# Folding softmax sums over partition quarters: a small product on TensorE, or two copies through DRAM

## The chip, the core and the metric

The kernel runs on one NeuronCore of a Trainium2 chip. The metric is the device time of one execution in microseconds (us); lower is better. PE is TensorE (matrix products), DVE VectorE, ACT ScalarE, POOL GpSimd, and SP is SyncE, which here issues nearly all of the copies between DRAM and on-chip memory.

## What is computed

Two layers over 16 batches of 1024 nodes with 256 channels, all in float32. Layer 0 is graph-weighted attention, layer 1 a two-step graph convolution; each ends in a residual sum and a layernorm. Cut to the first layer, for one batch:

```
c_adj = mean(x, channels)                          # one number for each node
A     = abs(abs(sigmoid(c_adj[m] - c_adj[n]) - 0.5) - 0.5) * 2
g     = relu((x.T @ (adj * A)) * para)             # 256 x 1024: the queries
k, v  = split(x @ kv_w)                            # 4 heads of 64 channels
attn  = softmax(q @ k.T * scale, axis=keys)
x     = layernorm(x + attn @ v)
```

and of the second layer

```
h = relu(x @ w1_loop + adj @ (x @ w1_neigh) + b1)
h = relu(h @ w2_loop + adj @ (h @ w2_neigh) + b2)
x = layernorm(x + (x + h) * 0.5)
```

The change is in the softmax's denominators, that is in the sums of exponentials over the keys.

## The kernel before, in words

A loop over the batches b = 0 to 15 (line 990) works on several batches at once: while batch b is in attention, the queries, keys and values of batch b + 1 are prepared, the first graph step of batch b - 1 and the second of batch b - 2 are done together (class Joined, lines 860 to 931), and batch b - 3 is normalized and stored. Batches 3 to 14 are all alike. Batch 0 and 1 lack the earlier batches, batch 2 lacks b - 3, and batch 15 has no next one. The order on every engine is the order of the calls (`tc.manual_schedule`, line 1159); no scheduler moves anything.

Attention goes in four units for each batch: a pair of heads and a half of the 1024 query nodes each. For a unit u:

- `scores(u)` (lines 586 to 607): eight times PE makes a tile of 128 keys by 2 x 512 scores (line 594), ACT takes the exponentials (597), and DVE adds the tile to `acc` (601, 603). DVE then transposes `acc` in blocks of 32 x 32 (605) and sums over 32 columns (607). This leaves `den_part`, 128 x 32: each denominator is still spread over four groups of 32 partitions, the quarters.
- `outputs(u)` (609 to 618): PE multiplies the exponentials with the values (614); DVE transposes the result to `o` (618).
- `add(u)` (620 to 639): PE multiplies `den_part` with the constant `fold`, which adds the four quarters and copies the sum to all of them (626); DVE takes two reciprocals from PSUM (630), multiplies `o` by them (632), adds the result to the residual `xB` (634) and sums it for the layernorm (635).

What lies between the units is written out by hand in `gap0`, `gap1`, `gap2` (lines 1005 to 1044). In the alike batches it is this, in the order of the calls:

- after unit 0, gap0: `means` (line 256) has ACT sum the next batch's nodes; the 1024 means go to DRAM as one line of 4-byte elements (263). `c1.inner` is a product (712). Then `add(0)`. SP loads the node form of batch b - 2 (`x<-x1d`, 705) and four blocks of a far adjacency form (`both.fetch(2, 3)`, line 181), POOL forms the operands R (882 to 885), and `row()` (268) reads the line of means back, broadcast to all partitions. DVE transposes the next batch's `xB` to `xT` (219).
- after unit 1's scores, DVE forms the key sums K (384 to 387).
- after unit 1, gap1: SP loads two row blocks of `adj` (443) and four more far blocks (`both.fetch(1, 4)`). `both.run` makes seven groups of products (892) in the order 1, 2, 6, 7, 5, 4, 3, with hooks between them: after group 2 DVE adds p1 (911) and does `add(1)`; after group 6 come a likeness on ACT (459, 460) and on DVE the moments of batch b - 3 (275, 276); after group 5 `weigh_first` on DVE (465, 518 to 521); after group 4's products DVE adds `uT` (925). The PSUM tile that line 925 reads is needed again by the second scores tile of unit 2.
- after unit 2, gap2: `c2.last` (780, 782 on PE; 787, 790 on DVE), then `add(2)`.
- after unit 3 the queries' products (546) with `add(3)` inside, then keys and values.

All of SP's copies of this part are on one queue. An instruction of SP that waits holds up all behind it. There are eight completion semaphores, used in turn: a copy is issued only once the copy eight places before it has landed.

Of the kernel before, what the change touches and what calls it, by code (L numbers as in the profile page):

```python
# [10 lines left out]
F32 = mybir.dt.float32  # L11
I32 = mybir.dt.int32
AF = mybir.ActivationFunctionType
ALU = mybir.AluOpType
AX = mybir.AxisListType
# [3 lines left out]
def kernel(  # L19
# [31 lines left out]
    nc = tc.nc  # L51

    B, N, C = x.shape
    P = 128
# [3 lines left out]
    HD = C // HEADS  # L58
    HID = w1_loop.shape[1]
    FB = 512  # L60
# [9 lines left out]
    S = 32  # L70
    NB = N // S
# [3 lines left out]
    Q = P // S  # L75
# [4 lines left out]
    small = ctx.enter_context(tc.tile_pool(name="small", bufs=4))  # L80
    psum = ctx.enter_context(tc.tile_pool(name="psum", bufs=2, space=bass.MemoryType.PSUM))

    dram = ctx.enter_context(tc.tile_pool(name="dram", bufs=2, space=bass.MemoryType.DRAM))
# [7 lines left out]
    def bank_psum(name):  # L91
        return psum.tile([P, FB], F32, tag="bank", name=name, bufs=2)
# [6 lines left out]
    def row_tile(name):  # L99
        return work.tile([P, N], F32, tag="row", name=name, bufs=ROWS)  # L100
# [15 lines left out]
    for t0 in range(0, NT, 2):  # L116
        nc.sync.dma_start(out=x_first[:, t0:t0 + 2, :],
                          in_=x[0, t0 * P:(t0 + 2) * P, :].rearrange("(t p) c -> p t c", p=P))
# [42 lines left out]
    fold = const.tile([P, Q, S], F32, name="fold")  # L161
# [14 lines left out]
    def fetch(n, name):  # L176

        rows = []
        for h in range(2):
            rows.append(row_tile(f"adj_{n}_{name}_{h}"))  # L180
            nc.sync.dma_start(out=rows[h], in_=far_adj[n][h])
        return rows

    def store(n, rows):
        for h in range(2):
            nc.sync.dma_start(out=far_adj[n][h], in_=rows[h])
# [28 lines left out]
    def channel_major(blocked, name):  # L215

        dst = work.tile([P, NC, N], F32, tag="xT", name=name, bufs=2)
        for cc in range(NC):
            nc.vector.transpose(dst[:, cc, :], blocked[cc])
        return dst  # L220
# [26 lines left out]
    def fold_sums(part, name):  # L247

        pm = bank_psum(f"{name}_ps")
        nc.tensor.matmul(pm[:, 0:NB], fold.rearrange("p a k -> p (a k)"), part[:, 0, :], start=True, stop=True)  # L250
        return pm[:, 0:NB]

    def join(part):
        nc.vector.tensor_add(part[:, 0, :], part[:, 0, :], part[:, 1, :])

    def means(q, xb, name):

        c_col = small.tile([P, NT], F32, tag="c_col", name=f"c_col_{name}", bufs=2)
        for t in range(NT):
            nc.scalar.activation(xb[:, t, :], xb[:, t, :], AF.Identity, accum_out=c_col[:, t:t + 1])  # L260
        nc.gpsimd.tensor_scalar_mul(c_col, c_col, 1.0 / C)
        line = dram.tile([1, N], F32, tag="line", name=f"line_{name}")
        nc.sync.dma_start(out=line.rearrange("o (t p) -> p (o t)", p=P), in_=c_col)
        q.c_col = c_col

        def row():
            q.c_row = work.tile([P, N], F32, tag="c_row", name=f"c_row_{name}")
            nc.sync.dma_start(out=q.c_row, in_=line.to_broadcast([P, N]))

        return row  # L270
# [24 lines left out]
    def by_node(t):  # L295
        return t.rearrange("p (bn r) -> p bn r", r=S)

    class BlockedNorm:


        def __init__(self, xB, sums, name):
            self.xB, self.sums, self.name = xB, sums, name

        def mean(self):
            mean = small.tile([P, NB], F32, tag="mean", name=f"mean1_{self.name}", bufs=2)
            nc.vector.tensor_scalar_mul(mean, fold_sums(self.sums, f"sum1_{self.name}"), 1.0 / C)
            for cc in range(NC):
                x_cc = by_node(self.xB[cc])
                nc.vector.tensor_sub(x_cc, x_cc, mean.unsqueeze(2).to_broadcast([P, NB, S]))  # L309
# [262 lines left out]
    class Attention:  # L572
# [5 lines left out]

        def __init__(self, b, xB, qT, kT, v):
            self.b, self.xB, self.qT, self.kT, self.v = b, xB, qT, kT, v  # L580
            self.part, self.o = {}, {}

            self.rden = small.tile([P, len(UNITS) * FB // S], F32, tag="rden", name=f"rden_{b}", bufs=2)
            self.sums = small.tile([P, NC, NB], F32, tag="sums", name=f"sums_{b}", bufs=2)
# [24 lines left out]
        def outputs(self, u):  # L609
# [7 lines left out]
            self.o[u] = work.tile([P, FB], F32, tag="o", name=f"o_{b}_{u}")  # L617
            nc.vector.transpose(self.o[u], pav)

        def add(self, u):  # L620

            b, (pair, j) = self.b, UNITS[u]
            half = FB // S
            pd = bank_psum(f"den_ps_{b}_{u}")
            den = pd[:, 0:2 * half]
            nc.tensor.matmul(den, fold.rearrange("p a k -> p (a k)"), self.part.pop(u), start=True, stop=True)
            rden = self.rden[:, ts(u, half)]
            for s in range(2):
                rows = slice(s * HD, (s + 1) * HD)
                nc.vector.reciprocal(rden[rows, :], den[rows, ts(s, half)])  # L630
            o = by_node(self.o.pop(u))
            nc.vector.tensor_mul(o, o, rden.unsqueeze(2).to_broadcast([P, half, S]))
            dst = by_node(self.xB[pair][:, ts(j, FB)])
            nc.vector.tensor_add(dst, dst, o)
            nc.vector.tensor_reduce(self.sums[:, pair, ts(j, half)], dst, AX.X, ALU.add)
            if u == len(UNITS) - 1:
                join(self.sums)
                nc.vector.tensor_reduce(rden_min[:, b:b + 1], self.rden, AX.X, ALU.min)
                nc.vector.tensor_reduce(rden_max[:, b:b + 1], self.rden, AX.X, ALU.max)
# [293 lines left out]
    def run():  # L933
# [56 lines left out]
        for b in range(B):  # L990
            more = b + 1 < B
            att = Attention(b, xB, qT, kT, v)
            c1, c2, c3 = (convs.get(b - k) for k in (1, 2, 3))
            both = Joined(c1, c2) if c2 else None
# [10 lines left out]
            def gap0():  # L1005
                row = means(q, xb, str(b + 1))
                c1.inner()
                att.add(0)
                if both:
                    c2.load_x()  # L1010
                    both.fetch(2, 3)
                    both.left(nc.gpsimd)
                row()
                ready["xT"] = channel_major(blocked, f"xT_{b + 1}")

# [5 lines left out]
            def gap1():  # L1021
                for t in (0, TJ):
                    q.load(t)
                if both:
                    both.fetch(1, 4)
                    both.run({1: (lambda: q.left(nc.gpsimd),),
                              2: (lambda: att.add(1),),
                              6: (lambda: q.likeness(0), lambda: c3 and c3.moments()),
                              7: (lambda: q.likeness(TJ),),
                              5: (weigh_first,),  # L1030
                              4: (lambda: c3 and c3.finish(out[b - 3]),),
                              3: (c1.turn_blocks,)})
                else:
                    q.left(nc.gpsimd)
                    for t in (0, TJ):
                        q.likeness(t)
                    store("01", rows01)
                    c1.first(rows01, lambda: (att.add(1), adj_sums(rows01, 1), adj_sums(rows01, 2), weigh_first()))
                    c1.turn_blocks()

            def gap2():
                if both:
                    c2.last()
                att.add(2)

            between = [gap0, gap1, gap2] if c1 and more else []
            if more:
                q = (FastQueries if c1 else Queries)(b + 1, xb)
            for u in range(len(UNITS)):
                att.scores(u)  # L1050
                if u == 1 and between:
                    kv = KeysValues(b + 1, ready["xT"])
                    kv.sums()
                if u == 3 and between:
                    for t in (2, TJ + 2, 3, TJ + 3):
                        q.load(t)
                    for t in (2, TJ + 2, 3, TJ + 3):
                        q.likeness(t)
                    q.right(1)
                if u and not between:  # L1060
                    att.add(u - 1)
                att.outputs(u)
                if u == 2 and more:
                    if c1:
                        for t in (1, TJ + 1):
                            q.load(t)
                            q.likeness(t)
                            q.times_adj(t)
                    else:
                        for t in range(3):  # L1070
                            q.load(t)
                            q.weigh(t)
                if u < 3 and between:
                    between[u]()
                if u == 0 and more and not between:
                    means(q, xb, str(b + 1))()
# [67 lines left out]
        both = Joined(c1, c2)  # L1144
# [83 lines left out]
```

## Time and profile before

| | us |
|---|---|
| median of 3 runs | 2168.85 (2168.66 to 2168.91) |
| the profiled execution's own time | 2169.0 |
| its span, from first to last instruction | 2167.2 |
| PE busy | 2153.0 (99%), in 8054 records |
| DVE busy | 1888.0 (87%) |
| ACT busy | 1033.0 (48%) |
| POOL busy | 367.3 (17%) |
| copies, mean | 132 GB/s, the queue of SP 54.9% of 16 engines' time |
| mean granted PE clock | 0.998 |

A float32 product is recorded as two instructions, so `x128` of line 626 are 64 calls. A row of the timeline gives the start, the time up to the end of the last merged instruction, the engine, the line and what is written from what; where an engine was idle before it, that and the releaser stand in brackets. A waiting SP is not idle in that sense: its waits are a view of their own. Matmul ends are modelled, so the time from one start to the next is the safer measure on PE. The time that a batch takes in the alike batches is 133.2 us, from the first scores at 801.32 to those at 934.52.

### The profile page before, as it was taken

How to read it: one execution, taken by the hardware profiler on the slowest of the kernel's cores; microseconds unless marked ns; L12 is line 12 of the kernel's file. 1: busy time of each engine (PE TensorE's matmuls, PEld its weight loads, DVE VectorE, ACT ScalarE, POOL GpSimd, SP SyncE). 2: the span in 40 equal slices, each digit the busy share in tenths (PEclk: the TensorE clock that was granted, in tenths of full speed). 3: DMA queues.
4: the chain of work that ended last, by engine and by line, in shares of the span. 5: the costliest groups of instructions: out<-in, count | busy, mean ns of one | idle time of the engine just before them, and what ended most of it. 6: DMA issues, size and time to landing. Idle time of an engine off the chain costs nothing.

```text
span 2167.2 us, 23089 instructions
## 1 busy us (share of the span) xinstructions
PE 2153.0 (99%) x8054; PEld 1024.8 (47%) x8054; DVE 1888.0 (87%) x2336; ACT 1033.0 (48%) x1356; POOL 367.3 (17%) x211
## 2 busy tenths in 40 slices
PE   9999999999999999999999999999999999999998
PEld 5344444544444444444444445454454444544354
DVE  5978998898998989989889888999989899898964
ACT  4744545545355453445444454445543445535412
POOL 1011130211303113030120301203022130221021
PEclk9999999999999999999999999999999999999999
DMA  9393663746556365473655536566374653743442
GB/s 240 107 136 117 135 161 99 132 140 118 146 128 152 112 125 156 125 170 95 115 163 124 163 88 115 172 122 155 98 114 163 122 156 109 121 152 82 120 136 99
DMA packets 611770, 286.21 MB, mean 132 GB/s; under 512 B 504768, under 2 KB 569152, under 8 KB 611648
## 3 DMA queue, kind: packets, MB, share of 16 engines
q1 hardware_dynamic: 611376, 284.15, 54.9%
q8 instruction: 65, 1.06, 0.2%
q14 instruction: 57, 0.47, 0.1%
q10 hardware_dynamic: 272, 0.52, 0.1%
HBM read 238.16 MB, written 46.46 MB: 131 GB/s over the span
## 4 chain that ended last, share of the span: by engine, by line


## 5 line engine op out<-in xcount | busy, mean ns | idle before, releaser
L597 ACT ACTIVATE pr<-s 128x1024 f32<-128x1024 f32 x512 | 476.1, 1051 | 176.6 <-PE s L594 176.6
L603 DVE TENSOR_TENSOR acc<-acc,pr 128x1024 f32<-128x1024 f32 x384 | 494.2, 1287 | 41.1 <-DVE acc L603 1.0
L594 PE MATMUL s<-qT,kT 64*128 64x512 f32 x2048 | 457.1, 596 | 0.7 <-ACT qT L480 0.7
L614 PE MATMUL av<-pr,v 128*64 128x512 f32 x2048 | 453.6, 595 | 0.0
L594 PEld LDWEIGHTS s<-qT,kT 64*128 64x128 f32 x2048 | 191.1, 186 | 236.1 <-ACT pr L597 111.5
L614 PEld LDWEIGHTS av<-pr,v 128*64 128x64 f32 x2048 | 141.2, 137 | 300.2 <-issue 285.8
L326 POOL TENSOR_TENSOR rstd<-rstd,neg_half 128x32 f32<-128x32 f32 x16 | 87.1, 5441 | 1111.5 <-DVE rstd L324 1111.5
L459 ACT ACTIVATE wg<-c_row,c_col 128x1024 f32<-128x1024 f32 x128 | 146.9, 1148 | 70.3 <-DVE accB L605 51.2
L465 DVE SCALAR_TENSOR_TENSOR wg<-wg,adj 128x1024 f32<-128x1024 f32 x128 | 149.8, 1209 | 11.3 <-ACT wg L460 10.4
L892 PE MATMUL hu_ps<-adj,R 128*128 128x512 f32 x360 | 158.3, 596 | 0.0
L460 ACT ACTIVATE wg<-wg 128x1024 f32<-128x1024 f32 x128 | 135.4, 1058 | 4.1
L314 ACT ACTIVATE sq<-xB_a 128x1024 f32<-128x1024 f32 x32 | 33.8, 1057 | 194.3 <-DVE xB_a L309 193.1
L360 PE MATMUL v_ps<-kvw_sb,xT 128*128 128x256 f32 x512 | 120.2, 379 | 0.1
L546 PE MATMUL g_ps<-wg,S 128*128 128x512 f32 x224 | 116.7, 603 | 0.0
L360 PEld LDWEIGHTS v_ps<-kvw_sb,xT 128*128 128x128 f32 x512 | 97.2, 190 | 38.4 <-issue 21.0
L546 PE MATMUL g_ps<-T,S 128*128 128x512 f32 x224 | 114.4, 592 | 0.0
L546 PE MATMUL g_ps<-wg,x 128*128 128x512 f32 x224 | 109.0, 599 | 0.0
L892 PE MATMUL hu_ps<-adjT,t 128*128 128x512 f32 x240 | 105.7, 592 | 0.0
L892 PEld LDWEIGHTS hu_ps<-adj,R 128*128 128x128 f32 x360 | 67.3, 190 | 78.9 <-issue 76.5
L601 DVE TENSOR_TENSOR acc<-pr,pr 128x1024 f32<-128x1024 f32 x64 | 76.9, 1201 | 23.7 <-ACT pr L597 23.7
L605 DVE STREAM_TRANSPOSE accB<-acc 128x1024 f32<-128x1024 f32 x64 | 79.7, 1246 | 3.2
L908 ACT COPY snap<-hu_ps 128x512 f32<-128x512 f32 x15 | 8.8, 586 | 150.3 <-PE hu_ps L892 150.3
(189 smaller groups left out, 2917.0 us busy)
## 6 DMA issues: line engine op xcount, KB each, us to landing
adj<-in_adj_dram SPq DMA_DIRECT2D x128, 512.0 KB, 3.9
adj<-adjT SPq DMA_DIRECT2D x120, 512.0 KB, 10.2
para<-in_L_gnn_para_dram SPq DMA_DIRECT2D x32, 512.0 KB, 3.4
xB_a<-in_x_dram SPq DMA_DIRECT2D x128, 128.0 KB, 4.2
x1d<-xB_a SPq DMA_DIRECT2D x128, 128.0 KB, 3.4
x<-x1d SPq DMA_DIRECT2D x16, 1024.0 KB, 16.6
xB<-in_x_dram SPq DMA_DIRECT2D x120, 128.0 KB, 4.3
x<-in_x_dram SPq DMA_DIRECT2D x15, 1024.0 KB, 6.9
```

What stands on the lines that cost most here:

```text
L326: nc.gpsimd.tensor_tensor(self.rstd, self.rstd, neg_half, ALU.pow)
L360: nc.tensor.matmul(pv[:, ts(i, C)], xT[:, cc, ts(g * per + i, P)], kvw_sb[:, cc, C:2 * C], start=(cc == 0), stop=(cc == NC - 1))
L459: nc.scalar.activation(wg, self.c_row, AF.Abs, bias=self.c_col[:, t:t + 1], scale=-1.0)
L460: nc.scalar.activation(wg, wg, AF.Tanh, scale=-0.5)
L465: nc.vector.scalar_tensor_tensor(wg, wg, 1.0, self.adj.pop(t), op0=ALU.add, op1=ALU.mult)
L546: nc.tensor.matmul(self.p[n], x_n[:, k, :], w_n, start=(k == 0), stop=(k == TJ - 1))
L594: nc.tensor.matmul(ps[:, ts(s, FB)], self.kT[rows, pair, ts(mt, P)], self.qT[rows, pair, ts(j, FB)], start=True, stop=True)
L597: nc.scalar.activation(pr, ps, AF.Exp)
L603: nc.vector.tensor_add(acc, acc, pr)
L605: nc.vector.transpose(accB, acc)
L614: nc.tensor.matmul(pav[s * HD:(s + 1) * HD, :], self.v[:, mt, pair * P + s * HD:pair * P + (s + 1) * HD], self.pr[mt][:, ts(s, FB)], start ...
L892: nc.tensor.matmul(dst, self.x[n][:, k, :], half_adj[w][:, k, :] if w else of_rows(rows, k), start=(start and k == 0), stop=(k == TJ - 1), ...
```

## The change

The fold product and the reading of its result from PSUM are gone. `spill(u)` writes `den_part` (16 KB) to DRAM; `fetch(u)` reads it back in four copies, one for each 32 partitions, so that each partition has the four quarters of its sum side by side (`quarters`, 128 x 4 x 16). `add(u)` sums them with one reduction on DVE and takes one reciprocal. A fetch waits for the landing of its spill. The three steps are called in different places, by unit:

- unit 0 of the batches with gaps: spill after the outputs, ahead of `means`; fetch after `both.fetch(2, 3)` and ahead of `row()`; `add(0)` moves from gap0 to after unit 1's scores, ahead of the key sums.
- unit 1: spill and fetch in gap1, after the loads of two `adj` blocks and after `both.fetch(1, 4)`; `add(1)` stays in its hook.
- unit 2: spill after the loads of two `adj` blocks, fetch at the start of gap2, `add(2)` after `c2.last` as before (in batch 1, which has no `both`, after unit 3's scores).
- unit 3: spill and fetch after the outputs, behind four loads of `adj`; `add(3)` stays.
- batches 0 and 15: spill and fetch right after each unit's outputs; the adds stay.

The tile `mean` of the layernorm has one buffer in place of two.

```diff
+        def spill(self, u):
+
+            self.far[u] = dram.tile([P, N // S], F32, tag="den", name=f"den_{self.b}_{u}", bufs=4)
+            nc.sync.dma_start(out=self.far[u], in_=self.part.pop(u))
+
+        def fetch(self, u):
+
+            self.quarters[u] = small.tile([P, Q, FB // S], F32, tag="quarters", name=f"quarters_{self.b}_{u}", bufs=2)
+            far = self.far.pop(u).rearrange("(a k) (s h) -> s k a h", k=S, s=2)
+            for a in range(Q):
+                nc.sync.dma_start(out=self.quarters[u][a * S:(a + 1) * S], in_=far[a * S // HD])
+
         def add(self, u):
 
             b, (pair, j) = self.b, UNITS[u]
             half = FB // S
-            pd = bank_psum(f"den_ps_{b}_{u}")
-            den = pd[:, 0:2 * half]
-            nc.tensor.matmul(den, fold.rearrange("p a k -> p (a k)"), self.part.pop(u), start=True, stop=True)
             rden = self.rden[:, ts(u, half)]
-            for s in range(2):
-                rows = slice(s * HD, (s + 1) * HD)
-                nc.vector.reciprocal(rden[rows, :], den[rows, ts(s, half)])
+            nc.vector.tensor_reduce(rden, self.quarters.pop(u).rearrange("p a h -> p h a"), AX.X, ALU.add)
+            nc.vector.reciprocal(rden, rden)
...
             def gap0():
                 row = means(q, xb, str(b + 1))
                 c1.inner()
-                att.add(0)
                 if both:
                     c2.load_x()
                     both.fetch(2, 3)
                     both.left(nc.gpsimd)
+                att.fetch(0)
                 row()
...
                 if both:
                     both.fetch(1, 4)
+                    att.spill(1)
+                    att.fetch(1)
                     both.run({1: (lambda: q.left(nc.gpsimd),),
                               2: (lambda: att.add(1),),
...
                 else:
+                    att.spill(1)
+                    att.fetch(1)
                     q.left(nc.gpsimd)
...
             def gap2():
+                att.fetch(2)
                 if both:
                     c2.last()
-                att.add(2)
+                    att.add(2)
...
             for u in range(len(UNITS)):
                 att.scores(u)
                 if u == 1 and between:
+                    att.add(0)
                     kv = KeysValues(b + 1, ready["xT"])
                     kv.sums()
...
-                if u and not between:
+                if u and (not between or u == 3 and not both):
                     att.add(u - 1)
                 att.outputs(u)
...
+                if not between or u != 1:
+                    att.spill(u)
+                if not between or u == 3:
+                    att.fetch(u)
                 if u < 3 and between:
                     between[u]()
```

More of the change, by code (lines that the diff above doesn't have):

```diff
@@ L304, in mean @@
         def mean(self):
-            mean = small.tile([P, NB], F32, tag="mean", name=f"mean1_{self.name}", bufs=2)
+            mean = small.tile([P, NB], F32, tag="mean", name=f"mean1_{self.name}", bufs=1)
             nc.vector.tensor_scalar_mul(mean, fold_sums(self.sums, f"sum1_{self.name}"), 1.0 / C)
@@ L580, in __init__ @@
             self.b, self.xB, self.qT, self.kT, self.v = b, xB, qT, kT, v
-            self.part, self.o = {}, {}
+            self.part, self.o, self.far, self.quarters = {}, {}, {}, {}
             self.rden = small.tile([P, len(UNITS) * FB // S], F32, tag="rden", name=f"rden_{b}", bufs=2)
```

## The prediction

> **What bounds the kernel now.** I first read the busy times of the page, then PE's waits, then the timelines of PE, SP and DVE over one of the alike batches (batch 6, scores from 801.32 to 934.52; batches 3 to 14 repeat it every 133.2 us), and last the copies' share in stretches.
>
> ```profile
> PE 2153.0 (99%) x8054; PEld 1024.8 (47%) x8054; DVE 1888.0 (87%) x2336; ACT 1033.0 (48%) x1356; POOL 367.3 (17%) x211
> ```
>
> PE is the bound, and its waits for others sum to 3.6 us (1.4 + 1.0 + 0.7 + 0.5). So what is taken from PE comes off the end, and what makes PE wait goes onto it. The PE timeline shows what a fold product costs:
>
> ```profile
> 835.23 7.03 PE L892 MATMUL hu_ps<-adjT,t 128*128 128x512 f32 x16
> 842.09 0.30 PE L626 MATMUL den_ps<-den_part,fold 128*128 128x32 f32 x2
> 842.23 10.55 PE L892 MATMUL hu_ps<-adj,R 128*128 128x512 f32 x24
> 852.62 3.60 PE L892 MATMUL hu_ps<-adj,h 128*128 128x512 f32 x8
> ...
> 861.29 7.14 PE L594 MATMUL s<-qT,kT 64*128 64x512 f32 x32
> ```
>
> 16 records take 6.86 us from start to start, 0.429 each. The next 24 should take 10.29 and take 10.39; with 0.14 for line 626 itself the fold costs 0.24. Next, SP's timeline:
>
> ```profile
> 809.18 1.44 SPq L749 DMA_DIRECT2D h<-h1d  x1
> 813.78 0.38 SPq L263 DMA_DIRECT2D line<-c_col  x1
> 814.26 0.53 SPq L705 DMA_DIRECT2D x<-x1d  x1
> 814.84 12.38 SPq L181 DMA_DIRECT2D adj<-adjT  x4
> 827.31 0.40 SPq L268 DMA_DIRECT2D c_row<-line  x1
> 827.80 1.03 SPq L443 DMA_DIRECT2D adj<-in_adj_dram  x2
> 830.61 7.21 SPq L181 DMA_DIRECT2D adj<-adjT  x4
> ```
>
> The copies in stretches (after the span: busy times by engine, granted clock, share of 16 DMA engines, GB/s):
>
> ```profile
> 814.00:826.00 12.00, 12.00 (x74) 7.15 (x70) 10.53 (x12) 6.52 (x8) 5.77 (x4) 1.00 0.37 20
> 826.00:843.00 17.00, 17.00 (x60) 6.72 (x57) 16.27 (x13) 2.52 (x4) 7.36 (x4) 1.00 0.99 378
> ```
>
> From 814 to 826 the queue moves 20 GB/s, because the line of 4-byte means (line 263) is at its head; the page puts its landing at 11.6 us. All behind it is then moved at 0.99 busy to 843. The last copy of the stage, issued at 837.50, lands 8.4 us later, at 845.9. And DVE:
>
> ```profile
> 816.30 1.22 DVE L607 TENSOR_REDUCE den_part<-accB 128x32 f32<-128x1024 f32 x1
> ...
> 844.64 0.51 DVE L630 RECIPROCAL rden<-den_ps 64x16 f32<-64x16 f32 x2
> ...
> 857.74 0.69 DVE L925 TENSOR_TENSOR uT<-snap,hu_ps 128x512 f32<-128x512 f32 x1
> ```
>
> From `add(1)` to the end of line 925, at 858.43, DVE has no gap: 13.8 us in order. The second scores tile of unit 2, on PE 0.97 after the first, at 862.25, needs line 925's PSUM tile. That slack of 3.8 us is the margin of everything below.
>
> [...] 1 MB of x issued at 814.26 crawls behind 4 KB. [...] Here the smallest landing of line 205's 256 KB stores is 2.0 us, their median 2.3. [...]
>
> **The change, part by part.**
>
> Removed on PE: 64 fold products. In the midst of 128-row products (`add(1)` of 14 batches, `add(3)` of 16) 30 x 0.23 = 6.9. Ahead of scores, 27 times: the start-to-start step of line 626 is 0.24, but the switch to 64-row tiles costs 0.09 without it too (799.50 to 801.32 is 1.82 where 1.73 is usual), so 27 x 0.15 = 4.0. Between scores and outputs in batches 0 and 15, 6 x 0.34 = 2.0. Batch 1's `add(2)` with its wait of 0.8: 1.2. Sum 14.1 us.
>
> DVE: 128 reciprocals at 251 ns against 64 reductions (nearest row: line 638's reduction of 128x64, 210 ns) and 64 reciprocals at about 250. That is 32.1 against 29.4 us, no cost. The single `mean` buffer costs nothing: a batch's mean is read 110 us before the next is written. The forming of K only moves behind `add(0)`; its reader is 60 us off.
>
> Added on SP: five issues for each unit, at 0.32 to 0.56 each, and two landings in a row. Their place decides, so I walk through batch 6.
>
> (1) spill(0) stands ahead of the line of means and waits for `den_part`, which ends at 817.5. The line goes out at about 818.0 in place of 813.78: 4.2 us later, and with it x, eight far blocks, c_row and two adj blocks. Since the stage runs at 0.99, it slides as a whole. The fetch's 512 pieces of 64 B add 0.4 (128-byte pieces move at about 150 GB/s, 1.2 a ns). The last far block lands at 845.9 + 4.6 = 850.5. Its own reader (group 4, from 852.6) is still served, and so are groups 6, 7 and 5.
>
> (2) `add(0)`: its quarters land behind the far blocks 2 and 3, near 841, where DVE could start near 836. K and line 911 follow to about 850. This wait hides behind the next one.
>
> (3) spill(1) stands behind all of these loads in the ring, so it lands about 0.7 after them (bounds 0.3 and 2.0), at 851.2. fetch(1) waits for that; four issues 1.3 (1.0 to 2.0); landing 2.1 (1.5 to 3.2): 854.6. With a slide of only 2.5 and the low ends it is 851; with the high ends 858. I take 854.6.
>
> (4) DVE waits in `add(1)`. Queued behind it are the moments, weigh_first and line 925, the 13.8 us. Line 925 ends at 868.4. PE, 0.38 us earlier than before by two folds, needs it at 861.9: it waits 6.5 us (2.9 to 9.9).
>
> (5) [...]
>
> (6) The rest of the batch: `add(2)` needs its quarters about 15 us after `den_part`, `add(3)` about 8 us after; two landings and four issues are about 6. Both are covered, by `c2.last`'s DVE work and by DVE's lines 518 to 521. If that cover is gone, the price is a few us of DVE, not of PE. Two more folds saved: -0.38.
>
> Net per alike batch: 868.4 - 862.25 = 6.1, + 1.5 - 0.4 = +7.2; 12 batches: +87.
>
> Others. Batch 2 has no moments (4.4 us less in the chain), and its line slides 5.2: wait about 3, net +3. Batch 0: the loads of adj 3 to 7 now stand behind spill(3) and fetch(3) and go out at 118 in place of 91 to 97; line 465 for block 3 runs at 122, not 117.4, PE waits about 4.7, net +5. Batch 1: -1. Batch 15: the loads of h and the far blocks stand behind fetch(3), near 2064 in place of 2028 to 2046; group 6 waits about 2.5, net +1.
>
> Sum: 87 + 3 + 5 - 1 + 1 = +95 against the profiled 2169.0 (span 2167.2 and 1.8 around it), which is 0.15 above the median. On the median: 2264.
>
> **The rivals.** *Gain*: fetch(1) lands by 848.1, so that line 925 is in time. It needs both that the stage doesn't slide (-4.2) and that the two landings take about 1 us each (-2.3). For it: 16 KB is little. Against it: ring order. Then -14.1 with some 5 to 8 of batches 0 and 15: 2162. The side turns where fetch(1) lands about 0.6 us after 848.1, since 12 waits of 0.6 with batches 0 and 15 eat the 14.1. *Mild*: the stage slides less, since x and the line overlap differently; quarters at about 850.4, wait 2.3, no clock loss: 12 x 1.5 + 8 = +26, 2195. *Worse*: landings at the high ends, half clock through unit 2 and a second wait at line 787 (0.6 us of slack there): 12 x 10.3 + 8 = +132, 2301. That the folds don't leave the path can't be: PE has no idle time around them.
>
> **How the numbers follow.** Chances: forecast 0.66, mild 0.16, gain 0.09, worse 0.09. The forecast's own range is 2215 to 2290. 2200 to 2295 leaves out the gain, about 0.05 of the mild and 0.06 of the worse case. A measurement of this kernel tells about 0.2% from no change: faster than 2164.5 has 0.08, within 0.2% 0.02, slower 0.90.
>
> **What would show it.** Right: the fold rows gone; line 263 issued 4 us later after the batch's first score; a DVE wait of some 6 us ahead of `add(1)`'s reduction on the quarters' landing; a PE wait at the second scores tile of unit 2 on line 925's twin; a granted clock below 1 in 12 batches; a period near 140.4. Wrong: quarters of unit 1 that land before DVE asks, or a DVE wait that ends without any on PE.

## The result, and the profile after

The changed kernel takes 2272.13 us (median of 4 runs, 2268.92 to 2274.29) against 2168.88 us (4 runs beside it): 1.0477 times as long, 95% interval 1.0463 to 1.0490. The forecast was 2264, with a range of 2200 to 2295.

The page of the profile after, first line:

```profile
PE 2179.9 (96%) x7926; PEld 1017.1 (45%) x7926; DVE 1848.3 (81%) x2336; ACT 1035.2 (46%) x1356; POOL 358.9 (16%) x211
```

PE has 128 records less, as 64 products of two records each should give, and still is busy 27 us longer: part of its work ran at a lower clock (mean granted clock 0.978 in this trace, 0.998 in that of before). The view of PE's waits says where the rest went (engine, line, what was waited for: us in total, times, longest):

```profile
PE s L594 <- DVE uT L933: 69.1, 13, 6.7
PE g_ps L473 <- DVE wg L465: 3.7, 1, 3.7
PE k_ps L350 <- DVE qT L479: 3.3, 1, 3.3
```

The first is the wait that was forecast, once in each of batches 2 to 14 (line 933 is line 925 of before, moved down by the new methods). The other two stand in batch 0.

Batch 6 now starts its scores at 835.83 (801.32 before), so 34.51 is to be taken off when these lines are held against those of before. SP's timeline:

```profile
852.07 0.34 SPq L623 DMA_DIRECT2D den<-den_part  x1
852.51 1.30 SPq L263 DMA_DIRECT2D line<-c_col  x1
853.90 0.53 SPq L713 DMA_DIRECT2D x<-x1d  x1
854.48 11.80 SPq L181 DMA_DIRECT2D adj<-adjT  x4
866.38 4.18 SPq L630 DMA_DIRECT2D quarters<-den  x4
...
875.66 1.99 SPq L181 DMA_DIRECT2D adj<-adjT  x4
877.74 0.38 SPq L623 DMA_DIRECT2D den<-den_part  x1
885.08 1.74 SPq L630 DMA_DIRECT2D quarters<-den  x4
```

The line of means goes out 16.68 us after the batch's start, where it was 12.46: 4.2 later, because the spill ahead of it waits for `den_part`. The spill of unit 1 is issued at 877.74, lands behind the last far block at 885.06, and only then its fetch may go. All 1203 of SP's copies in this trace land in the order of their issue, and of the 1195 with a copy eight places before them none goes out ahead of its landing (76 within 0.1 us of it). DVE's timeline of the same batch:

```profile
876.42 0.26 DVE L637 TENSOR_REDUCE rden<-quarters 128x16 f32<-128x64 f32 x1 [5.67 <-DMA quarters<-den]
...
888.33 0.26 DVE L637 TENSOR_REDUCE rden<-quarters 128x16 f32<-128x64 f32 x1 [5.46 <-DMA quarters<-den]
...
901.35 0.68 DVE L933 TENSOR_TENSOR uT<-snap,hu_ps 128x512 f32<-128x512 f32 x1
```

and PE's:

```profile
891.91 3.60 PE L900 MATMUL hu_ps<-adjT,R 128*128 128x512 f32 x8
895.43 1.13 PE L594 MATMUL s<-qT,kT 64*128 64x512 f32 x4
902.08 7.87 PE L594 MATMUL s<-qT,kT 64*128 64x512 f32 x28 [5.52 <-DVE uT L933]
```

Where before one row showed the eight scores tiles of unit 2 without a break, the first tile stands alone now, and PE waits 5.52 us for line 933. From `add(1)` at 888.33 to the end of line 933 at 902.03 DVE works in order for 13.7 us, as long as before; it only starts so late that the slack of 3.8 us is used up and 5.5 us are missing. The stretches around it (after the span: PE, PEld, DVE, ACT, POOL busy, granted clock, share and GB/s of the copies):

```profile
895.00:897.00 2.00, 1.56 (x6) 0.30 (x4) 1.93 (x5) 1.08 (x2) 1.42 (x1) 1.00 0.00 0
899.00:901.00 2.00, 0.00 (x0) 0.00 (x0) 1.90 (x3) 0.00 (x0) 0.49 (x1) 0.50 0.00 0
903.00:906.00 3.00, 3.00 (x12) 1.28 (x10) 3.00 (x8) 1.31 (x2) 0.00 (x0) 0.61 0.13 45
```

The granted clock falls to 0.50 within the wait and is still down when PE has work again (0.50 from 898.51 to 905.34).

Cutting every batch at PE's first scores record of each unit gives the account (batches 3 to 14, means):

| stretch | before | after | what it is |
|---|---|---|---|
| unit 0 to unit 1 | 18.00 | 17.85 | fold gone |
| unit 1 to unit 2 | 41.97 | 41.84 | fold gone; small waits in four batches |
| first to second scores tile of unit 2 | 0.97 | 6.75 | the wait |
| from there to unit 3 | 20.36 | 22.56 | fold gone, clock down |
| unit 3 to the next batch | 51.90 | 51.93 | fold gone, a new wait of 0.16, in three batches 0.35 more |
| period | 133.20 | 140.92 | +7.7 |

Twelve of these are 92.7 us. Batch 0 adds 10.95 (99.74 to 110.69), batch 2 adds 2.0, batch 15 adds 0.4; batch 1 gives 0.8 back.

### The profile page after: what moved, and what is told of

The parts are those of the page before. It is cut to its first block, busy times and chain, and to the rows that moved or that the text cites. A ratio compares the mean times of both kernels' runs of the same rounds, so it can differ in the third digit from the quotient of the medians.

```text
span 2272.3 us, 23249 instructions
## 1 busy us (share of the span) xinstructions
PE 2179.9 (96%) x7926; PEld 1017.1 (45%) x7926; DVE 1848.3 (81%) x2336; ACT 1035.2 (46%) x1356; POOL 358.9 (16%) x211
## 4 chain that ended last, share of the span: by engine, by line
## 5 line engine op out<-in xcount | busy, mean ns | idle before, releaser
L594 PE MATMUL s<-qT,kT 64*128 64x512 f32 x2048 | 487.3, 626 | 69.7 <-DVE uT L933 69.1
L594 PEld LDWEIGHTS s<-qT,kT 64*128 64x128 f32 x2048 | 200.2, 196 | 332.0 <-issue 112.3
L637 DVE TENSOR_REDUCE rden<-quarters 128x16 f32<-128x64 f32 x64 | 16.3, 254 | 149.9 <-DMA quarters<-den 149.9
L601 DVE TENSOR_TENSOR acc<-pr,pr 128x1024 f32<-128x1024 f32 x64 | 82.3, 1286 | 37.0 <-ACT pr L597 37.0
L281 POOL TENSOR_TENSOR rstd_g<-rstd_g,neg_half 128x8 f32<-128x8 f32 x15 | 35.8, 2387 | 322.3 <-DVE rstd_g L280 322.3
```

The source lines that it names most:

```text
L594: nc.tensor.matmul(ps[:, ts(s, FB)], self.kT[rows, pair, ts(mt, P)], self.qT[rows, pair, ts(j, FB)], start=True, stop=True)
L601: nc.vector.tensor_add(acc, self.pr[0], pr)
```

## The experiments

Times are medians, ratios are to the kernel before run beside them. "Period" is the mean of batches 3 to 14 in the trace, which is of one of the runs. A wait at the second scores tile of unit 2 is given as the time from the first tile to the second, less the 0.97 us that it takes without a wait.

**add(1) behind uT.**

```diff
-                              2: (lambda: att.add(1),),
...
                               3: (c1.turn_blocks,)})
+                    att.add(1)
```

> The changed kernel with one call moved: add(1) of the batches with a joined step goes from the hook after group 2 to the end of gap1, behind line 933's twin and turn_blocks. Copies, queue and landings stay. Theory (DVE's order makes the late quarters a PE wait): uT is then ready before PE asks, as in the kernel before; no wait at the second scores tile, no loss of clock, a period of about 132.8 in place of 140.9; 2272 - 12 x 8.1 - 2 = 2173, what is left being batch 0. Rival (the landings or the moved add(0) alone make uT late, since add(0) already waits 5.7 us on DVE): a PE wait of 2 us or more stays, period 135 or more, 2200 or more.

Measured: 2173.72 us, ratio 1.0026 (1.0017 to 1.0035), period 133.10. The copies land as late as in the changed kernel, but PE's timeline shows unit 2's scores in one row again:

```profile
861.88 3.60 PE L900 MATMUL hu_ps<-adjT,R 128*128 128x512 f32 x8
865.40 7.14 PE L594 MATMUL s<-qT,kT 64*128 64x512 f32 x32
872.47 7.09 PE L614 MATMUL av<-pr,v 128*64 128x512 f32 x32
```

and DVE's, that uT is done before `add(1)` and nothing waits for the quarters:

```profile
862.24 0.68 DVE L933 TENSOR_TENSOR uT<-snap,hu_ps 128x512 f32<-128x512 f32 x1
...
867.40 0.22 DVE L637 TENSOR_REDUCE rden<-quarters 128x16 f32<-128x64 f32 x1
```

So one place in DVE's order is worth 98 us, 94 of them in the twelve alike batches. The rival falls: neither the landings nor the moved `add(0)`, which still waits here, makes uT late by itself. What is left above 2169 is batch 0, which takes 106.88 us here.

**The means ahead of the spill.**

```diff
                 row = means(q, xb, str(b + 1))
+                att.spill(0)
                 c1.inner()
...
-                if not between or u != 1:
+                if not between or u > 1:
                     att.spill(u)
```

> The changed kernel with the spill of unit 0 one place later on SP's queue: behind the line of means instead of ahead of it. Theory (4.2 us of the lateness are the line's, which the spill holds up, and the two landings in a row are the rest): the line goes out 4.2 us earlier, the last far block and both quarters land about 4 us earlier, the wait at the second scores tile falls from 5.8 to about 1.6 us and the clock stays up; period about 134.6, total 2272 - 12 x 6.3 - 2 = 2194. Rival (the two landings behind the full ring are all of it and the place of the line doesn't matter, since the stage is bound by its bytes): period stays at 140 to 141, total 2265 to 2275.

Measured: 2192.34 us, ratio 1.0107 (1.0090 to 1.0124), period 134.32; the wait at the second tile is 1.2 us on average (1.6 were expected), from none to 2.7. The clock was expected to stay up; after one of these waits, of 2.26 us, it didn't (granted 0.50 for 3.41 us, shown in the last section). SP's timeline:

```profile
823.60 0.38 SPq L263 DMA_DIRECT2D line<-c_col  x1
827.37 0.34 SPq L623 DMA_DIRECT2D den<-den_part  x1
...
847.98 0.59 SPq L623 DMA_DIRECT2D den<-den_part  x1
855.26 1.74 SPq L630 DMA_DIRECT2D quarters<-den  x4
```

The batch starts at 811.14, so the line is back at 12.46, and the fetch of unit 1 goes out at 44.1 where the changed kernel has 49.25. The rival falls: the order of two small copies moves the period by 6.6 us.

**Unit 1 on ACT's queue.**

```diff
-                    att.spill(1)
-                    att.fetch(1)
+                    att.spill(1, nc.scalar)
+                    att.fetch(1, nc.scalar)
```

> The changed kernel with unit 1's spill and fetch, in the batches with a joined step, issued by ACT instead of SP, so that they stand in another ring and not behind the far blocks. The line of means stays late. Theory (it is ring order that makes unit 1's quarters late): quarters of unit 1 land within 5 us of den_part, before DVE asks; the wait at the second scores tile is 0 to 0.5 us (add(0) alone uses up the slack of 3.8), period about 133, total 2272 - 12 x 7.9 - 2 = 2175. Rival (two landings cost this much on any queue while the engines are full): quarters still land late, period 137 to 141.

Measured: 2227.94 us, ratio 1.0263 (1.0245 to 1.0281), period 137.01. Neither forecast holds. The quarters land 48.0 us after the batch's start, 4.3 earlier than in the changed kernel, and the wait at the second scores tile is gone, as the theory said. But they land 13.1 us after `den_part` and not within 5: with the 16 engines at 0.85 of their time, the spill takes 4.2 us from issue to landing and the last fetch 5.9. Two things changed at once here: ACT also issues the spill 36.4 us after the batch's start, where SP, held up by its own waits, came to it at 41.9 (in batch 6). So what the place on SP's queue alone costs is not told by this run. It shows the quarters 4.3 us earlier, and a spill of 16 KB that still takes 4.2 from issue to landing. And ACT's timeline shows a new price (ACTq are its copies):

```profile
863.55 0.34 ACTq L623 DMA_DIRECT2D den<-den_part  x1
867.75 1.99 ACTq L630 DMA_DIRECT2D quarters<-den  x4
869.84 0.58 ACT L916 COPY snap<-hu_ps 128x512 f32<-128x512 f32 x1 [16.21 <-DVE xB_a L642]
```

and PE's timeline who pays it:

```profile
870.52 12.15 PE L900 MATMUL hu_ps<-adj,R 128*128 128x512 f32 x24 [2.57 <-issue]
```

The releaser in the brackets of line 916 is only the latest event before it. ACT sits in front of its fetch until the spill has landed, its copy of p1 stands behind that, and PE's group 6, which writes the PSUM tile that p1 is copied from, waits 2.6 us. Then its 24 records take 12.15 and not 10.46. The wait has moved from DVE's queue to ACT's.

**The gap filled.**

```diff
             for mt in range(NT):
+                if fill and mt == 1:
+                    spare = bank_psum(f"spare_{b}")
+                    for _ in range(6):
+                        nc.tensor.matmul(spare, ident, self.kT[:, 0, 0:FB], start=True, stop=True)
...
-                att.scores(u)
+                att.scores(u, fill=u == 2 and between and both)
```

> The changed kernel with six products of 128x512 whose result nobody reads, between the first and the second scores tile of unit 2 in batches 2 to 14: 12 x 0.43 = 5.2 us of PE work inside the wait of 5.8. DVE, copies and the moment at which uT is ready stay. Theory (2.35 us of the 7.7 per batch are the lowered clock after the gap): the clock stays at 1, unit 2 after its second tile takes 20.2 us and not 22.6, period about 138.6, total 2272 - 12 x 2.35 = 2244. Rival (the slower rest of unit 2 comes from ACT and DVE that run late, not from the clock): total 2268 to 2276. If the six products come on top of the wait, it is slower by up to 12 x 5.

Measured: 2248.85 us, ratio 1.0372 (1.0355 to 1.0389): 23 us faster with 78 products more. PE's timeline (the lines of the kernel are shifted by four):

```profile
889.83 1.13 PE L598 MATMUL s<-qT,kT 64*128 64x512 f32 x4
890.89 5.42 PE L594 MATMUL spare<-kT,ident 128*128 128x512 f32 x12
896.49 6.28 PE L598 MATMUL s<-qT,kT 64*128 64x512 f32 x28 [0.18 <-DVE uT L937]
```

The second tile comes 6.57 us after the first (6.75 without the filling), so uT is as late as ever; from there to unit 3 it is 20.33 in every batch and not 22.56. That difference, 2.23 us a batch, is the clock: keeping PE at work is all that was changed, and the mean granted clock of the run goes from 0.978 to 0.997 (1.00 from 890 to 903, the stretch of this batch's filling). 12 x 2.4 = 29 come off the alike batches; batch 2, whose wait is only 1.6, pays 4.3 for its filling.

**The two costs apart and together.** Three kernels with the one before as their base; the second and the third also have the changed kernel's single `mean` buffer. The first only makes the line of means late:

```diff
             def gap0():
+                far = dram.tile([P, N // S], F32, tag="den", name=f"den_{b}", bufs=4)
+                nc.sync.dma_start(out=far, in_=att.part[0])
                 row = means(q, xb, str(b + 1))
```

> The kernel before with one thing added: in gap0, ahead of the line of means, SP copies den_part of unit 0 to a DRAM tile that nobody reads. All folds stay products, all adds stay in their places. It puts the 4.2 us delay of the line, and of all loads behind it, into the kernel by itself. Theory (the late stage costs nothing by itself, since each far block still lands before its group; it costs only through the quarters behind it): the last far block lands near 850 in place of 845.9 from the batch's old start, PE waits 0 to 0.2 us a batch; total 2169 to 2172. Rival (the late loads alone hold up PE's groups): 1 us a batch or more, 2181 or more.

Measured: 2169.66 us, ratio 1.0004 (0.9995 to 1.0012), period 133.23. The line goes out at 16.67, the last far block lands at 47.2 to 48.2 after the batch's start (43.8 to 45.0 in the four batches of before where that landing is recorded), and PE doesn't notice.

The second folds only unit 1 by copies:

```diff
                 if both:
                     both.fetch(1, 4)
+                    att.spill(1)
+                    att.fetch(1)
                     both.run({1: (lambda: q.left(nc.gpsimd),),
```

> The kernel before with only unit 1 of batches 2 to 14 folded by copies, called as in the changed kernel; units 0, 2 and 3 and all of batches 0, 1 and 15 keep the product, add(0) stays in gap0, the line of means keeps its place. Theory (two landings in a row behind the far blocks): the stage ends on time, quarters land about 849.3 from the old start (845.9 + 0.3 + 3.1), DVE, which could start at 844.6, starts at 849.5 and ends uT at 863.3; PE, 0.2 earlier, needs it at 862.0: wait 1.3, less 0.2 for the fold; no loss of clock; total 2169 + 12 x 1.1 = 2182. Rivals: the late line or the moved add(0) is the real cause, then 2166 to 2169; the clock falls even in gaps this small, then 2190 or more.

Measured: 2170.39 us (20 runs, 2168.56 to 2176.03), ratio 1.0011 (1.0004 to 1.0018), period 133.16. I had expected 2182, and a wait of 1.3, and neither rival's time came either; the wait is 0.8 and 0.6 in batches 3 and 4 and next to none in the ten others. (The trace is of the quickest of the 20 runs, so the median run probably waits in more batches.) DVE waits for the quarters,

```profile
848.44 0.26 DVE L644 TENSOR_REDUCE rden<-quarters 128x16 f32<-128x64 f32 x1 [2.79 <-DMA quarters<-den]
```

but starts 46.2 after the batch's start, not 48.2. I had taken the landing of the last far block from batch 6 of the trace before (44.57), which is one of the later ones; here the spill lands at 43.0 to 44.5. uT is done at 59.9 to 61.5, and PE asks at about 60.7: this kernel sits on the edge of the slack, which fits the scatter of its runs. The single `mean` buffer, which no run tests alone, is in this kernel too and so can't cost much.

The third has both edits:

> The fifth and the sixth experiment in one kernel: the kernel before with unit 1 of batches 2 to 14 by copies, and the unread copy of den_part ahead of the line of means; add(0) stays in gap0 with its product. Each alone cost under 0.1 us a batch. Theory (both eat the same slack of 3.8 us, so that they cost nothing apart and much together): unit 1's quarters land near 852.7 from the old start, DVE ends uT at 866.7, PE waits 4.7 at the second scores tile and loses 1.5 to 2.3 of clock; period 139, total 2169 + 12 x 6 = 2241, with 2215 to 2255. Rival (costs add, and it is the moved add(0) that makes the changed kernel slow): 2169 to 2173.

Measured: 2247.85 us, ratio 1.0369 (1.0353 to 1.0385), period 139.17. PE waits 4.1 us at the second tile in the alike batches, and from there to unit 3 it is 22.39 and not 20.36; the trace is of the quickest of the four runs (2241.35 us), so the others lose somewhat more. DVE in the same place:

```profile
871.53 0.26 DVE L644 TENSOR_REDUCE rden<-quarters 128x16 f32<-128x64 f32 x1 [8.03 <-DMA quarters<-den]
```

Two edits that cost 0.8 and 1.6 us apart cost 79 together, with `add(0)` where it always was. The late line alone stays inside the slack of 3.8 us, unit 1's copies alone just use it up, and the two together go beyond it. The rival falls.

**Batches 0 and 15 by the product.**

```diff
-                if not between or u != 1:
+                if between and u != 1:
                     att.spill(u)
-                if not between or u == 3:
+                if between and u == 3:
                     att.fetch(u)
```

with the product of before kept in `add` for a unit that was never spilled.

> The changed kernel with the product kept in batches 0 and 15, which have no gaps; batches 1 to 14 as changed. Theory (batch 0 lost 11 us because spill(3) and fetch(3) hold back the loads of adj 3 to 7, of 20 blocks for batch 1 and of para, all on SP's queue): batch 0 takes 99.7 us again in place of 110.7, batch 15 gives back 0.4, total 2272 - 11 = 2261. Rival (the loss of batch 0 comes from the order of its adds or from a batch that starts late and catches up): 2266 or more.

Measured: 2253.91 us, ratio 1.0399 (1.0381 to 1.0416). Batch 0 takes 99.74 us again. The rest of the 18 us is not from this edit alone: the alike batches happen to have a period of 140.3 here.

**All three repairs.** `add(1)` behind turn_blocks, spill(0) behind the means, unit 3 of batches 0 and 15 by the product; every other unit by copies.

> Three repairs together: add(1) at the end of gap1 (as in the first experiment), spill(0) behind the line of means (as in the second), unit 3 of batches 0 and 15 by the product; all other units by copies. Theory (the folds' 14 us are real and all that took their place were waits on copies): batches 2 to 14 at about 132.6 in place of 133.2, batch 1 at 116.1, batches 0 and 15 about 0.6 shorter each; total 2168.9 - 13 x 0.6 - 0.5 - 0.7 - 1.3 = 2159, with 2157 to 2163 for small new waits. Rival (the gain is taken by new waits wherever the copies stand): 2166 or more.

Measured: 2162.46 us, ratio 0.9971 (0.9960 to 0.9983), period 132.89. Faster than before and inside the range of 2157 to 2163, but 3.5 us short of 2159. Batch 0 takes 99.04 us, with its units 0 to 2 by copies: so it was unit 3's copies, and not any fold by copies, that made it slow in the changed kernel. Units 0, 1 and 2 give 0.15, 0.22 and 0.14 back; unit 3 gives none, since the first products of the next keys wait 0.36 us in sum, the second of them for DVE's line 558, which still reads its PSUM tile.

**The same with add(1) one step earlier.**

```diff
-                              4: (lambda: c3 and c3.finish(out[b - 3]),),
+                              4: (lambda: c3 and c3.finish(out[b - 3]), lambda: att.add(1)),
                               3: (c1.turn_blocks,)})
-                    att.add(1)
```

> The eighth kernel with add(1) one step earlier: in the hook after group 4, behind uT and the normalization of batch b - 3, ahead of turn_blocks. DVE idles 1.84 us there for h1T, and add(1) takes 2.6. Theory (DVE runs late into the tail of the batch and the second key product waits 0.2 to 0.4 us for its line 558): DVE gains up to 1.8 us, the wait shrinks, 2159 to 2161. Rival (the wait at the key products comes from a chain that starts at add(3), so DVE's earlier work doesn't matter): 2162 to 2163, no difference.

Measured: 2159.91 us (5 runs, 2159.65 to 2160.22), ratio 0.9961 (0.9947 to 0.9974), period 132.69. The wait at the key products is down to 0.16, as the theory said, and the rival falls. This is the fastest version here: 8.7 us below the kernel before run beside it. None of its PE waits is for a copy of the fold or for uT.

## Why the prediction was right, point by point

- **Removed on PE, 14.1 us.** Right in kind: unit 0 gives 0.15 (0.15 said), unit 1 0.22 where it isn't held up (0.23), unit 2 0.14 (0.15). Unit 3 was said to give 0.23; PE has gained 0.22 after the fold's place, but 0.16 is lost again at the keys. Of 14.1 us the best kernel here keeps 8.7.
- **Line of means 4.2 later.** Measured 4.2.
- **The stage slides as a whole, last far block at 850.5.** In batch 6 884.87, which is 850.4 on the old scale.
- **K and line 911 to about 850.** 882.86, or 848.4.
- **Unit 1's quarters at 854.6.** Spill landed at 850.6 (851.2 said), fetch at 853.6.
- **PE waits 6.5 (2.9 to 9.9).** 5.8 on average, since both landings were a little quicker than I took: the spill landed 0.2 after the last far block (0.7 said), the last fetch 1.75 after its issue (2.1 said). On an idle queue the spill of unit 2 landed in 1.4 (issued at 917.41, the copy before it landed at 916.79).
- **Clock, +1.5 in the net per alike batch.** This was my estimate, and no trace of before showed such a loss. Measured 2.2, by the filled gap: 0.7 too small, where the wait was 0.7 too large. That these two cancel is luck. The 0.5 between the 7.2 that was said and 7.7 is the four folds: 0.76 was said to come back, and 0.3 did, since small new waits took the rest.
- **Batches 1, 2 and 15.** -0.8, +2.0, +0.4 (-1, +3, +1 said).
- **Batch 0, +5. This step failed.** It took 10.95 more. I wrote that "the loads of adj 3 to 7 now stand behind spill(3) and fetch(3)", and priced the wait for block 3 at 4.7. It is there, with 3.75. But the same queue has 20 blocks for batch 1 (line 210) and the two loads of `para` behind those, and I left them out. SP's row for `para` in the kernel before:

```profile
122.61 1.32 SPq L449 DMA_DIRECT2D para<-in_L_gnn_para_dram  x2
```

and SP's timeline in batch 0 of the changed kernel:

```profile
113.71 0.34 SPq L623 DMA_DIRECT2D den<-den_part  x1
115.14 1.73 SPq L630 DMA_DIRECT2D quarters<-den  x4
116.98 2.57 SPq L443 DMA_DIRECT2D adj<-in_adj_dram  x5
119.65 23.08 SPq L210 DMA_DIRECT2D adjB<-in_adj_dram  x20
142.77 1.12 SPq L449 DMA_DIRECT2D para<-in_L_gnn_para_dram  x2
```

and PE's:

```profile
122.24 5.40 PE L473 MATMUL g_ps<-wg,x 128*128 128x512 f32 x8 [3.75 <-DVE wg L465]
...
148.60 6.57 PE L350 MATMUL k_ps<-xT,kvw_sb 128*128 128x512 f32 x8 [3.34 <-DVE qT L479]
```

`para` goes out 20.2 us later than before, DVE's line 479 waits for it, and PE for that: 3.3 more. After each of the two gaps 8 records take 5.40 and 6.57 where rows of 8 elsewhere take 3.60, and the granted clock is 0.50 from 123.7 to 127.1 and 0.51 from 147.5 to 154.5: some 5 us of clock come on top, an estimate from these stretches. The size is not fixed: in the traces of the first four experiments, whose batch 0 has the same instructions, it costs 7.1 to 10.1. With the 6 us of the twelve alike batches it is what the forecast of 95 lacks against the 105 of the traced run. With the product in batches 0 and 15 all of it is gone.

The mechanism of the 12 alike batches is shown from three sides: without DVE's order it doesn't cost (first experiment), without the late line it costs a seventh, 1.1 of 7.7 us a batch (second), and it can be put together from two edits that cost next to nothing apart (ninth). That the order of SP's queue alone (ring order in the texts before the runs) makes unit 1's copies late is only partly shown: on another queue they came 4.3 us earlier, not the 8 us that "within 5 us of den_part" would have been, and part of that is the earlier issue. The rival "gain" was nearer than I thought: I asked for no slide of the stage and quicker landings too, and the sixth experiment, which has only the first, is already at the edge.

## What to carry to other kernels

Before a wait goes onto a queue, find the slack of the first thing behind it that another engine needs, and add up all that draws on it: here 3.8 us carried either of two delays for less than 2 us, and both for 79. The place of a small copy counted here, not its bytes (16 KB landed in 1.4 us on an idle queue and in 7.3 behind the far blocks): put it behind the copy that feeds the long chain, and put the work that waits for it behind the work that PE needs. When a step is moved on a queue, list every instruction behind it to the end of the stage, not only the next.

## What the runs showed that I had not expected

**What a wait costs in clock depends on where it falls.** Take the waits at the second scores tile in the changed kernel, with the idle time that the view puts in brackets, and hold the time from that tile to unit 3 against the 20.33 us of batch 2. Batch 2's wait of 1.62 us cost nothing; the twelve others, of 4.34 to 6.72, cost 1.54 to 2.95, without getting dearer with length: the longest cost 2.53, the shortest of the twelve 2.80, and one of 6.31 the 1.54.

The clock records of the changed kernel's trace show the order behind this. All 15 falls of the granted clock (from 1.00 to 0.50) lie on one raster of 3.413 us, to within 1 ns, and a low stretch lasts one (once), two (12 times) or three (once) of its steps, but for the one that the end of the kernel cuts off. Whether the clock fell went with the step just before: in the 15 steps ahead of a fall PE was idle for 1.91 us or more, in every other step at full clock for 1.77 or less. Two waits of other runs agree. The one of 2.26 us, in PE's timeline of the second experiment, lies in one step:

```profile
1141.83 4.40 PE L594 MATMUL s<-qT,kT 64*128 64x512 f32 x12 [2.26 <-DVE uT L933]
```

The steps of that trace's raster there (the first number after the comma is PE's busy time, the granted clock is the third from the end):

```profile
1139.57:1142.98 3.41, 1.15 (x7) 0.68 (x8) 3.31 (x8) 1.02 (x1) 0.00 (x0) 1.00 0.00 0
1142.98:1146.39 3.41, 3.41 (x10) 1.40 (x10) 3.41 (x7) 2.17 (x3) 0.00 (x0) 0.50 0.31 106
1146.39:1149.80 3.41, 3.41 (x18) 1.23 (x16) 3.10 (x4) 3.41 (x4) 0.00 (x0) 1.00 0.99 257
```

A wait of 3.3 us in the ninth experiment, after which the granted clock stayed at 1.00, is split by the raster of its trace into 1.39 and 1.93 (3.41 less the busy time of the first two steps):

```profile
1721.49 2.85 PE L594 MATMUL s<-qT,kT 64*128 64x512 f32 x12 [3.32 <-DVE uT L940]
```

```profile
1716.15:1719.56 3.41, 2.02 (x7) 0.44 (x5) 3.38 (x4) 1.71 (x2) 2.75 (x2) 1.00 0.00 0
1719.56:1722.97 3.41, 1.48 (x8) 0.77 (x10) 3.32 (x9) 0.30 (x1) 0.00 (x0) 1.00 0.00 0
1722.97:1726.38 3.41, 3.41 (x20) 1.46 (x16) 3.31 (x6) 3.41 (x5) 0.00 (x0) 1.00 0.41 137
```

So it was not the length of a wait alone that told, but how much of it fell into one step, and a step need not have been idle throughout: 1.91 and 1.94 of 3.41 us came before a fall in the changed kernel, 1.93 did not in the ninth experiment. Figures that close can't be told apart, since PE's idle time rests on modelled ends, and no run here moved the raster on purpose.

**The key sums took 1 us less each.** Two of the four lines that form K are far shorter in their new place. DVE's groups of instructions (after the bar: busy time, mean ns), first of the kernel before:

```profile
L385 DVE TENSOR_TENSOR K<-xT 128x512 f32<-128x512 f32 x14 | 23.5, 1681 | 0.0
```

then of the changed kernel:

```profile
L385 DVE TENSOR_TENSOR K<-xT 128x512 f32<-128x512 f32 x14 | 9.6, 684 | 0.0
```

Before, POOL's lines 507 and 508 run beside them (838.80 to 842.12 in batch 6); after, POOL is idle then. In the kernel before, batch 1 has no work of POOL beside its lines 385 and 386, and there each takes 0.68 too. Why they are shorter is not shown: no run here changed POOL's work alone, and line 384, which overlaps line 507 for 0.5 of its 0.68 us in batch 6, is not longer. The two lines lose 27.8 us and the additions to `xB` 12.4 (mean 885 ns before, 692 after); that is the size of the 40 us that DVE is busy less. It bought nothing, since DVE then waits for the quarters all the same.
